# Four blocks of the second image's attention weights turned by TensorE instead of by a trip through DRAM

## The chip, the cores and the metric

The kernel runs on one core of a Trainium2 chip. The metric is the device time of one execution in microseconds (us), the median over several runs. A core has TensorE (PE, matrix products), VectorE (DVE), ScalarE (ACT), GpSimd (POOL) and SyncE (SP, which here only issues transfers), and 16 DMA engines that all queues share. Matrix products write PSUM banks of 128 x 512 floats; DVE, ACT and POOL carry results on.

## The reference, cut to what matters

Two images of 128 channels x 64 x 64 pixels, that is 4096 tokens of 128 channels each, go through a neighbourhood-attention layer (layer 0) and then through layer 1, whose first half is full self-attention in which queries, keys and values are the same normalised tokens:

```python
sim = jnp.einsum('blh,bmh->blm', q, q) * scale
sim = jnp.where(diag[None, :, :], jnp.float32(-1000000000.0), sim)
attn = jax.nn.softmax(sim, axis=-1)
return jnp.einsum('blm,bmh->blh', attn, q)
```

The second half of layer 1 is a spectral convolution: filters `phi`, branch matrices `M_phi_plus` and `M_phi_minus` (four branches of 16 matrices of 128 x 128 each, mixed with weights from a softmax) and `M_u` for three short lags. All of it is in float32.

## The kernel before, in words

**Order.** Layer 0 of both images comes first, in an order written out by a planner. Then `attention(0, fill)` and `attention(1, fill)` do the self-attention of the first and of the second image, and the convolution's long loop ends the kernel. This case lies in `attention(1)`, at about 800 to 1250 us of the profile.

**Pairs of chunks.** The 4096 tokens are cut into 8 chunks of 512. Since queries and keys are the same tokens, the block of exponentials E for queries in chunk a and keys in chunk c is the transpose of the block for queries in c and keys in a. So only the 36 pairs with a <= c are computed. For a pair off the diagonal, `weights` computes four row tiles of 128 x 512 (scores on PE in L927 or L936, exponential on ACT in L932 or L943); then
- `other` (L1057): E itself, contracted over the tokens of a, is added to the result of chunk c;
- `own` (L985): E transposed, contracted over the tokens of c, is added to the result of chunk a. This needs E turned.

**Two ways to turn.** A "far" pair is turned by way of DRAM: ACT issues one 1 MB store `eb<-e` (`sent`, L959), two steps later SP issues four loads `et<-eb` of 256 KB (`moved`, L966), which put 32 x 32 blocks into place, and DVE turns inside the blocks with two stream transposes of 128 x 1024 (`turned`, L975). The four `own` products follow eight steps after the store (`DELAY`). The pair (6, 7), the last one, is not far: after each of its four `other` products PE turns four 128 x 128 tiles into a PSUM bank (`turned_here`, L981), DVE copies the bank out (L982), and `own` follows one step later.

**Steps and fillers.** A pair off the diagonal takes four steps. In a step PE does a score product for the next pair, an `other` product of this pair and up to two `own` products that are due (`late`, a first-in first-out list), and `fill()` adds one piece of unrelated work. The order is written by hand for PE, DVE, ACT, POOL and SP: nothing is reordered at run time. In the second image the fillers are, in this order: what is left of the first image's tokens (`after`: it ends with 12 stores `us<-ub` per chunk, four of 128 KB and eight small ones of 32 KB, L1094, each after an addition on POOL, L1141); whenever a chunk is complete, `after` for that chunk; and `for_ffn`, which loads the branch matrices (`filter_matrices`: 32 loads `st` of 256 KB, issued by SP at L1277 about three ahead of use and added up on DVE in L1299 and L1301), then the table `inv` (320 KB, L1499, scaled on DVE in L1501) and the first blocks `ct` and `ut` of the convolution (L1459, L1467).

**Completion counters.** The framework gives each DMA one of eight completion counters in turn; SP's and ACT's DMAs draw from the same eight. Before a queue issues a DMA it waits until the DMA that last held this counter has landed. So a store on SP may have to wait for an `eb` store of ACT that drew the same counter.

**Buffers.** `e` and `et` have two buffers each (1 MB), `eb` four, the PSUM ring `bank` five, `own` two, `other` one.

Of the kernel before, what the change touches and what calls it, by code (L numbers as in the profile page):

```python
# [92 lines left out]
CHUNKS = (0, 1, 4, 5, 2, 3, 6, 7)  # L93
# [9 lines left out]
def kernel(  # L103
# [136 lines left out]
    with l0a:  # L240
# [551 lines left out]
        for k, (b, g) in enumerate(order):  # L792
            t = {}
# [83 lines left out]
    with ap_:  # L877
# [24 lines left out]
        def attention(b, fill):  # L902
# [8 lines left out]


            pairs = [(a, c) for a in range(8) for c in range(a, 8)]
            far = lambda a, c: a != c and (a, c) != (6, 7)
            chunk = lambda a: slice(CHUNKS[a] * 512, (CHUNKS[a] + 1) * 512)

            def weights(a, c, k, left, halves):
# [66 lines left out]
            def onto(own, n, out_, e, first, last):  # L984
                nc.tensor.matmul(out_, lhsT=tok[b][:, n, :], rhs=e, start=first, stop=last, skip_group_check=True)  # L985

            def complete(a, own):
                xs = xa[b][:, chunk(a)]
                if a:
                    nc.vector.tensor_tensor(xs, own, xs, ALU.add)  # L990
                else:
                    nc.vector.tensor_copy(xs, own)
                fill(CHUNKS[a])

            def pair_onto(own, a, c, et, t):
                if (a, c) == (6, 7):
                    onto(own, 4 * CHUNKS[c] + t, own, et[:, t], False, t == 3)
                    if t == 3:
                        complete(a, own)
                    return  # L1000
                onto(
                    own, 4 * CHUNKS[c] + t, own.rearrange("p (k q i) -> p q k i", k=4, q=4),
                    et.rearrange("p q (k t i) -> p t q k i", k=4, t=4)[:, t], False, c == 7 and t == 3,
                )
                if (c, t) == (7, 3):
                    complete(a, own)
# [11 lines left out]
            def pass_on(n):  # L1018

                while coming_ and coming_[0][0] + MOVE <= step:  # L1020
                    at, eb, a, c = coming_.pop(0)
                    et = moved(eb)
                    turns.append((at + TURN, et))
                    late.extend((at + DELAY, a, c, et, t) for t in range(4))
                while turns and turns[0][0] <= step:
                    turned(turns.pop(0)[1])
                while n and late and late[0][0] <= step:
                    _, a, c, et, t = late.pop(0)
                    pair_onto(owns[a], a, c, et, t)
                    n -= 1  # L1030
# [409 lines left out]
        kept = []  # L1440
        fill, left = filler(0, steps, kept)
        attention(0, fill)
        for gen in steps:
            for _ in gen:
# [63 lines left out]
        kept = []  # L1508
        fill, left = filler(1, steps, kept)
        attention(1, fill)  # L1510
        adder[:] = [nc.vector]
        for gen in steps:
# [23 lines left out]
    with ExitStack() as cv:  # L1536
# [201 lines left out]
        b = NB - 1  # L1738
# [117 lines left out]
```

## Time and profile before

| | us |
|---|---|
| median of 3 runs | 2059.06 (2057.91 to 2060.68) |
| the profiled execution | 2061.56 |
| its span, first to last instruction | 2059.8 |
| PE busy | 1924.6 (93%) |
| DVE, ACT, POOL busy | 941.0, 733.1, 570.6 |
| TensorE clock granted, mean | 0.971 of full |

The span is the time from the first to the last instruction of the profiled execution; 1.8 us of that execution lie around it. Matrix products overlap at their ends, so a stretch in which PE is "busy" is not free of small gaps, but an idle time in front of a product, which the timeline shows in brackets with its releaser, is real. In a timeline a product of 128 x 512 floats is two instructions (x2), which start 0.86 us before the next product does when PE is not held up.

### The profile page before, as it was taken

What the parts mean: (1) busy time and instruction counts of PE and PEld (TensorE: products, weight loads), DVE (VectorE), ACT (ScalarE), POOL (GpSimd) and SP (SyncE); (2) the same over time, 40 slices, a digit from 0 to 9 for tenths busy, and PEclk for the clock granted to TensorE, in tenths of its full rate; (3) what the DMA queues carried; (4) which work ended last, traced back from release to release, by engine and by line L of the source; (5) the groups of instructions that cost most, each with busy time, mean ns of one, the idle gap of its engine ahead of it and who ended that gap; (6) DMA issues with size and microseconds to landing.
All of it is one profiled execution on the core that took longest, in us unless ns stands there. A gap on an engine that the chain in (4) does not pass through costs nothing.

```text
span 2059.8 us, 50961 instructions
## 1 busy us (share of the span) xinstructions
PE 1924.6 (93%) x20504; PEld 1355.8 (66%) x20504; DVE 941.0 (46%) x2918; ACT 733.1 (36%) x1718; POOL 570.6 (28%) x954
## 2 busy tenths in 40 slices
PE   6899998999899999897978898999999999999998
PEld 4677775444444444443433344799999899999987
DVE  5799995443544343242533336333333334333332
ACT  3789885312223323222312232222222222222222
POOL 4467986303422113101101111022222121222211
PEclk8999999999999999999989999999999999999999
DMA  5222221667656534648865632222222123222211
GB/s 153 62 62 62 62 58 31 191 149 232 188 154 178 159 108 150 172 119 209 226 173 160 182 112 73 70 68 67 66 67 60 51 56 103 68 66 67 67 45 43
DMA packets 278378, 225.97 MB, mean 110 GB/s; under 512 B 122607, under 2 KB 241535, under 8 KB 270720
## 3 DMA queue, kind: packets, MB, share of 16 engines
q1 hardware_dynamic: 269442, 162.59, 32.1%
q10 hardware_dynamic: 8126, 58.04, 7.0%
q8 instruction: 163, 2.67, 0.5%
q0 software_dynamic: 576, 2.10, 0.3%
q14 instruction: 71, 0.58, 0.1%
HBM read 131.40 MB, written 91.25 MB: 108 GB/s over the span
## 4 chain that ended last, share of the span: by engine, by line
PE 75%; DVE 8%; DMA 5%; POOL 4%; issue 4%; ACT 1%; SPq 1%; DVEq 0%; POOLq 0%; ACTq 0%
PE acc L1584 27%; PE own L985 10%; PE bank L927 7%; PE pc L1565 7%; PE other L1057 6%; PE bank L349 2%; PE bank L559 2%; PE bank L202 2%; PE bank L1156 2%; DMA et<-eb 2%; PE bank L1199 1%; DMA eb<-e 1%; DVE et L975 1%; PE bank L523 1%; PE po L581 1%
## 5 line engine op out<-in xcount | busy, mean ns | idle before, releaser
L1570 DVE COPY y<-pc 128x512 f32<-128x512 f32 x320 | 206.1, 686 | 347.4 <-PE pc L1565 345.9
L1584 PE MATMUL acc<-y,mpl 32*128 32x256 f32 x5120 | 324.9, 380 | 0.8 <-DVE af L1594 0.8
L1584 PE MATMUL acc<-y,mmi 32*128 32x256 f32 x5120 | 316.5, 375 | 0.0
L1570 ACT COPY y<-pc 128x512 f32<-128x512 f32 x320 | 171.9, 589 | 392.7 <-PE pc L1565 379.1
L1584 PEld LDWEIGHTS acc<-y,mpl 32*128 32x128 f32 x5120 | 289.9, 186 | 8.3 <-DVE af L1594 1.3
L1584 PEld LDWEIGHTS acc<-y,mmi 32*128 32x128 f32 x5120 | 290.9, 185 | 3.9
L985 PE MATMUL own<-et,tok 128*128 128x512 f32 x448 | 225.9, 629 | 61.2 <-DVE et L975 49.1
L932 ACT ACTIVATE e<-bank 128x512 f32<-128x512 f32 x216 | 128.8, 599 | 308.0 <-PE bank L927 302.7
L1057 PE MATMUL other<-e,tok 128*128 128x512 f32 x448 | 230.9, 597 | 6.5 <-DVE xa L1066 6.5
L927 PE MATMUL bank<-cm 128*128 128x512 f32 x432 | 227.3, 608 | 0.0
L1565 PE MATMUL pc<-ct,ut 32*128 32x256 f32 x2560 | 212.5, 377 | 3.1 <-DVE y L1570 3.1
L1595 POOL TENSOR_TENSOR af<-af 128x512 f32<-128x512 f32 x39 | 49.7, 1275 | 589.2 <-DVE af L1594 589.2
L985 PEld LDWEIGHTS own<-et,tok 128*128 128x128 f32 x448 | 86.9, 199 | 177.5 <-issue 108.7
L1565 PEld LDWEIGHTS pc<-ct,ut 32*128 32x128 f32 x2560 | 172.7, 186 | 9.3 <-DVE y L1570 5.2
L975 DVE STREAM_TRANSPOSE et<-et 128x1024 f32<-128x1024 f32 x108 | 127.7, 1221 | 67.6 <-DMA et<-eb 66.3
L174 POOL TENSOR_TENSOR ln_rs<-ln_rs,mhalf 128x4 f32<-128x4 f32 x24 | 25.3, 1054 | 480.6 <-DVE ln_rs L173 480.5
L1057 PEld LDWEIGHTS other<-e,tok 128*128 128x128 f32 x448 | 81.6, 191 | 100.0 <-issue 84.0
L1141 POOL TENSOR_TENSOR ub<-uo 128x256 f32<-128x256 f32 (+1 forms) x160 | 96.5, 640 | 178.1 <-ACT uo L1138 167.5
L927 PEld LDWEIGHTS bank<-cm 128*128 128x128 f32 x432 | 76.9, 194 | 73.5 <-issue 67.8
L546 ACT ACTIVATE p<-p,mn 128x196 f32<-128x196 f32 x256 | 114.4, 449 | 14.4 <-DVE mn L536 13.8
L1138 ACT COPY uo<-bank 128x512 f32<-128x512 f32 (+1 forms) x96 | 46.9, 517 | 125.3 <-PE bank L1156 96.6
L943 ACT ACTIVATE e<-bank 128x512 f32<-128x512 f32 (+1 forms) x72 | 32.6, 455 | 139.0 <-DVE bank L941 133.9
(261 smaller groups left out, 2559.7 us busy)
## 6 DMA issues: line engine op xcount, KB each, us to landing
eb<-e ACTq DMA_DIRECT2D x54, 1024.0 KB
et<-eb SPq DMA_DIRECT2D x216, 256.0 KB
ut<-us SPq DMA_DIRECT2D x160, 128.0 KB
us<-ub SPq DMA_DIRECT2D x128, 128.0 KB
ct<-gs SPq DMA_DIRECT2D x320, 40.0 KB
vw<-vd SPq DMA_DIRECT2D x256, 49.0 KB
ct<-gs SPq DMA_DIRECT2D x320, 32.0 KB
vd<-v SPq DMA_DIRECT2D x128, 32.0 KB
```

The costliest lines, as they stand in the source:

```text
L546: nc.scalar.activation(p, p, AF.Exp, bias=t[name + "mn"][:, h : h + 1], scale=-1.0, accum_out=t["den"][:, u, h : h + 1],)
L927: nc.tensor.matmul(ps.rearrange("p (q t j) -> p q t j", q=4, t=4), lhsT=cm[b][:, n * P : (n + 1) * P], rhs=keys.rearrange("p (t q j) -> p ...
L932: nc.scalar.activation(e, ps.rearrange("p (q r) -> p q r", q=4), AF.Exp, bias=0.0, scale=ASCALE)
L975: in_place(nc.vector.transpose(flat, flat))
L985: nc.tensor.matmul(out_, lhsT=tok[b][:, n, :], rhs=e, start=first, stop=last, skip_group_check=True)
L1057: nc.tensor.matmul(turn(other, "p (q r) -> p q r"), lhsT=tok[b][:, n, :], rhs=es[j], start=(j == 0), stop=(j == 3),)
L1138: nc.scalar.copy(both[:, 0 : 2 * n], pu[s][:, 0 : 2 * n])
L1141: adder[0].tensor_tensor(ub[:, sgn, 0:n], both[:, 0:n], both[:, n : 2 * n], op)
L1565: nc.tensor.matmul(pcs[j].rearrange("p (g o c) -> p o g c", g=4, o=2)[:, :, at], lhsT=ut[rows_, par, :], rhs=cv_[rows_], start=True, stop= ...
L1570: (nc.scalar.copy if j % 2 else nc.vector.tensor_copy)(y[:, :, :, 4 * kl + j, :], pcs[j].rearrange("p (g x k) -> p k g x", g=4, k=KF))
L1584: nc.tensor.matmul(acc[j][:, 0:256], lhsT=(mmi if l else mpl)[rows_, k, :], rhs=y[rows_, k, 2 * l : 2 * l + 2].rearrange("p s n x -> p (s ...
L1595: eng.tensor_tensor(af[:, 0:2], af[:, 0:2], af[:, 2:4], ALU.add)
```

## The change

The set of pairs that are turned on the spot grows, for the second image only. `pairs[9:27:3]` are the entries 9, 12, 15, 18, 21 and 24 of the list of pairs: (1, 2), (1, 5), (2, 2), (2, 5), (3, 3) and (3, 6). The pairs (2, 2) and (3, 3) are on the diagonal and were never far, so four pairs change their way: (1, 2), (1, 5), (2, 5) and (3, 6). For each of them the `eb` store, the four `et` loads and the two stream transposes go, and 16 turns of 128 x 128 on PE and four copies of 128 x 512 on DVE come. Their `own` products come one step after each turn, or as soon as an older far pair in `late` has been served, instead of eight steps after a store; scores and exponentials are laid out in plain order.

```diff
             pairs = [(a, c) for a in range(8) for c in range(a, 8)]
-            far = lambda a, c: a != c and (a, c) != (6, 7)
+            here_ = {(6, 7), *(pairs[9:27:3] if b else ())}
+            far = lambda a, c: a != c and (a, c) not in here_
...
             def pair_onto(own, a, c, et, t):
-                if (a, c) == (6, 7):
-                    onto(own, 4 * CHUNKS[c] + t, own, et[:, t], False, t == 3)
-                    if t == 3:
+                if not far(a, c):
+                    onto(own, 4 * CHUNKS[c] + t, own, et[:, t], False, c == 7 and t == 3)
+                    if (c, t) == (7, 3):
                         complete(a, own)
                     return
```

The second hunk lets pairs other than (6, 7) go that way: the sum of chunk a is closed only by its last pair, the one with c = 7.

## The prediction

> **What bounds the kernel now.** I read the page first (PE is busy for 93% of the span, so PE sets the time wherever it isn't kept waiting), then the table by stage, to see where it is kept waiting. Columns: stage, its length, busy us (x instructions) of PE, PEld, DVE, ACT, POOL, granted clock, DMA share, GB/s.
>
> ```profile
> 940.00:1020.00 80.00, 65.69 (x167) 29.61 (x166) 36.16 (x67) 20.53 (x44) 3.15 (x4) 0.94 0.83 214
> 1020.00:1070.00 50.00, 35.76 (x104) 16.01 (x103) 19.57 (x31) 10.50 (x24) 5.52 (x10) 0.86 0.74 195
> 1070.00:1110.00 40.00, 32.11 (x80) 14.14 (x79) 16.96 (x39) 11.06 (x23) 2.64 (x3) 0.87 0.51 151
> 1110.00:1150.00 40.00, 32.27 (x98) 14.56 (x97) 7.99 (x13) 7.56 (x15) 6.01 (x11) 0.90 0.63 172
> ```
>
> In these 210 us, the middle of the second image's attention, PE is idle for 44 us and the DMA engines are at their busiest. PE's timeline shows where: four long stalls, each in front of an `own` product on a turned block: **A** at 949.8 (11.46 us), **B** at 1038.7 (12.44), **C** at 1095.5 (6.85), **D** at 1139.7 (7.16). What ends them stands in the chain of work that ended last (start, us, what):
>
> ```profile
> 949.59 5.10 DMA eb<-e
> 955.72 3.10 DMA st<-in_m_plus_dram
> 959.99 1.22 DVE et L975
> 961.25 3.58 PE own L985 x4
> ...
> 1038.50 3.88 DMA eb<-e
> 1045.58 3.15 DMA st<-in_m_minus_dram
> 1049.87 1.22 DVE et L975
> 1051.13 3.78 PE own L985 x4
> ...
> 1092.38 6.62 DMA inv<-t_out
> 1100.01 2.28 DVE et L975 x2
> 1102.34 3.78 PE own L985 x4
> ...
> 1118.70 5.12 DMA eb<-e
> 1136.77 3.88 DMA et<-eb
> 1140.67 6.21 DMA ct<-gs
> 1146.88 3.77 PE own L985 x4
> ```
>
> The reader is to see that A and B wait not for the turned block but for a branch matrix: DVE stands at `mpl` or `mmi` (L1299) until `st` lands, and the stream transposes are queued behind it. `st` is late because SP is. The waits of SP from 940 to 1150:
>
> ```profile
> SPq L1094 <- DMA eb<-e: 28.5, 5, 6.7
> ```
>
> SP's small `us` stores share completion counters with ACT's `eb` stores. In the listing of waits of the built program, one of A's last stores has the counter of (1, 6)'s `eb`, issued at 949.59; one of B's has that of (2, 6), and one of the last three that of (2, 7), issued at 1038.50. In A: `eb` lands at 954.7, SP goes on, `st` is issued at 955.3 and lands at 958.4, DVE needs 0.5 and 2.4 us, PE starts at 961.25. C waits for `inv`, queued on SP behind the four loads of (3, 5). In D the loads of (3, 7) are queued behind 15 `ct` and `ut` loads, and these behind a store with the counter of (3, 7)'s `eb` (1118.70).
>
> Each stall also costs the clock: after B four products take 3.57 us from start to start and not 1.72, the next 1.71 and not 0.86: about 2.8 us with the rest; the same after C and D, 1.7 after A.
>
> **What the Trainium skill says.** (1) "TensorE: Matmul & The Clock Gate", Part 1: an idle window of about 3.4 us halves the clock; the products at twice their time after A to D agree. (2) The same page, Part 4: a turn on PE ends in PSUM and needs a DVE copy. The trace agrees: 273 ns for a turn, and each bank is copied in 686 ns; back to back the turns cost less, as the next fence shows. (3) "DMA: Bandwidth & Descriptors", Issuing engines are not separate DMA queues: transfers of ACT and SP run on the same 16 engines. That fits the loads and stores that overlap here, and is why I expect fewer bytes to help a little, but none of the four stalls is a lack of bandwidth alone.
>
> **The change part by part.** PE, DVE, ACT, SP (POOL's order is unchanged; so is all of the first image):
>
> *Added on PE:* 4 pairs x 16 turns. Four of them take 0.43 us of PE (start to start):
>
> ```profile
> 1230.91 0.60 PE L981 MATMUL bank<-ident,e 128*128 128x128 f32 x4
> 1231.34 0.81 PE L936 MATMUL bank<-cm 128*128 128x384 f32 x2
> ```
>
> 16 x 0.43 = **6.9 us**, less the last 0.4 us of (1, 5), which fall into stall A: **+6.5**. Nothing hides the rest, as PE is the bound.
>
> *Added and removed on DVE:* 16 copies x 0.686 = 11.0 us against 8 stream transposes x 1.214 = 9.7 us. DVE is busy for under half of these stages, so the time itself is covered by PE's; but each copy stands in DVE's order, with an `own` product behind it, and a fifth of the PSUM ring is held until it is done. In (2, 5) and (3, 6) each step then takes four banks of the five rather than three. No row shows this; the nearest is the last pair, where turns on the spot made PE wait 1.42 us once (1241.8). Bounds: 0 (no wait) to 16 steps x 0.25 us = 4; below nothing it can't be. I take **+1.5**.
>
> *Removed from the queues:* ACT loses 4 issues of 0.33 us, SP 16 of 0.43 us = 6.8 us. Both queues have idle time, so this counts only through what it lets pass. *Removed from the DMA engines:* 4 x 2 MB. The scores and exponentials stay as many, of the same size.
>
> *Stall A:* in the new order of waits (1, 6)'s `eb` again holds the counter of a small `us` store, now the last but one of the chunk. The stall stays: `eb` may land 1.2 us sooner (3.8 us after (1, 1), when the engines were quiet, against 5.1), but one more issue (0.55) and one copy of (1, 5) (0.6) now lie between it and PE. I take **-0.5**, bounds -3 and +2.
>
> *Stall B:* in the new order none of the 12 stores of that chunk draws an `eb`'s counter; (2, 6)'s `eb` falls behind them and its next holder is a load of its own block. So `st` no longer waits for (2, 7). POOL's last addition ended at 1027.5 there; eight issues of 0.55 us, 0.9 us of shift and a landing of 3.2 us give about 1036, where DVE waits, with only the sum of (2, 6), due at 1040, behind it. The pair for which PE waited, (2, 5), is turned by PE itself. **-12.44 - 2.8 = -15.2.** What could be late next is C.
>
> *Stall C:* (3, 5) stays far, `inv` stays behind it. Only (3, 6)'s `eb` (issued at 1095.38) leaves the engines while `inv` lands: **-1**, bounds 0 and -9.6 (all of it and the clock).
>
> *Stall D:* no `us` store draws (3, 7)'s counter now; a `ct` load does, 6 issues later, when that `eb` has landed. `ct` starts about 4.2 us sooner (1123 and not 1127.2), and so do the four loads of (3, 7) at 1136.77; with (4, 5)'s `eb` of 1139.52 no longer beside them they should land some 3 us faster than the 7.6 us they took. Both together are as much as the stall: **-7.16 - 2.7 = -9.9**, bounds -3 and -9.9.
>
> Sum: 6.5 + 1.5 - 0.5 - 15.2 - 1 - 9.9 = **-18.6 us** on the profiled execution's 2061.56, so 2043.0; the median of the runs lies 2.5 us under that execution: **2040.5**.
>
> **The rivals.**
> 1. *B and D go, A and C stay* (as above): 2040.5; with the bounds of its terms 2036 to 2053. For it: the counters in the listing and the landing times fit A, B and D to a tenth of a us.
> 2. *Bandwidth was the cause, and A and C go too:* 2 MB less in every third pair. It would bring up to 13.2 + 9.7 us more, less the 1.5 counted: some 2019; half of it 2030. For it: the DMA share of 0.83 from 940 on. Against: from 945.5 to 949, just ahead of A, the engines move 15 to 46 GB/s, the small stores alone.
> 3. *The stall moves:* B's work comes 15 us sooner, the branch matrices don't, and DVE stops at another `st` or at `inv` with a copy or a transpose behind it. Then C grows by up to what B and D lose: 2052 to 2059. For it: DMA share 0.74 with PE stalled; it must run the same loads in less time.
> 4. *Slower:* the copies are the new wait. Every turned pair has its four `own` products behind DVE copies, and DVE stands at L1299 or L1301 for `st`; if in (2, 5) and (3, 6) it stands as long as before, B and D survive with PE waiting for a copy, and the turns (6.9) and the ring (4) are paid for nothing: 2070. It decides once the stalls shrink by less than 8 us in sum. Against: in the new DVE order the copies of (2, 5) stand ahead of the `mmi` at which B stood.
> 5. *It doesn't do what it says:* six entries are picked and two are diagonal pairs; the built program shows 64 more turns, 16 fewer loads and 4 fewer stores, so four pairs are changed.
>
> **How the numbers follow.** Chances: rival 1 0.61, rival 2 0.15, rival 3 0.13, rival 4 0.11. A measurement of this kernel can tell about 0.2%, 4.1 us, from no change. Rivals 1, 2 and two thirds of 3 are faster by more: 0.84; a third of 3 is within: 0.05; slower 0.11. The range leaves out rival 4 and the far half of rival 2: 2027 to 2057.
>
> **What would show it right or wrong.** In the profile after: 96 turns on the spot (32 now), `et<-eb` x200, `eb<-e` x50. A stall of 10 to 12 us at the end of (1, 5), still ended by `st` and behind SP's wait for an `eb`; none over 3 us after (2, 6); one of 5 to 7 us ended by `inv` after (3, 5); at most 3 us after (4, 4). SP's wait of L1094 for `eb` falls from 28.5 to under 15 us. I am wrong if PE waits for L982 for more than 5 us in sum, if B comes back under another `st`, or if A is gone too.

## Result: 2050.6 us against 2058.3, less than half of the forecast gain

In runs taken in turn on one chip the kernel before had a median of 2058.3 us (2055.95 to 2060.68) and the changed kernel 2050.63 us (2048.89 to 2054.29): a ratio of **0.996, 95% interval 0.9947 to 0.9973**, that is 7.7 us less. The forecast was 18.6 us less. The profiled execution of the changed kernel took 2050.63 us, its span is 2048.9 us, and PE's granted clock is 0.977 (before: 0.971). Behind the edited line the numbers of the changed kernel's lines are one higher: L985 of the kernel before is L986, L1094 is L1095; some experiments move them again.

**The same four stages after the change** (columns as before: stage, length, busy us of PE, PEld, DVE, ACT, POOL, granted clock, DMA share, GB/s):

```profile
940.00:1020.00 80.00, 65.76 (x179) 30.24 (x177) 35.96 (x68) 18.91 (x41) 1.45 (x1) 0.94 0.70 185
1020.00:1070.00 50.00, 45.44 (x146) 21.36 (x143) 22.94 (x35) 13.98 (x30) 7.22 (x12) 1.00 0.69 182
1070.00:1110.00 40.00, 32.02 (x105) 14.66 (x104) 13.88 (x36) 11.88 (x26) 7.78 (x11) 0.87 0.46 127
1110.00:1150.00 40.00, 34.96 (x91) 16.27 (x90) 11.02 (x19) 6.28 (x13) 0.88 (x3) 0.91 0.55 147
```

The second stage is another one: PE busy for 45.4 us and not 35.8, at the full clock. That is where B was. In the fourth, where D is, PE is busy for 35.0 us and not 32.3. In the first stage the DMA share falls from 0.83 to 0.70, and PE is busy for 65.8 us against 65.7 before: the fewer bytes brought nothing there.

**The stalls.** PE's timeline (start, us, what, and in brackets the idle time just before it and its releaser; x4 are four instructions, two products of 128 x 512, which the prediction calls four products) has these left in place of A to D:

```profile
963.45 3.78 PE L986 MATMUL own<-et,tok 128*128 128x512 f32 x4 [11.38 <-DVE et L976]
1033.72 1.98 PE L986 MATMUL own<-et,tok 128*128 128x512 f32 x4 [0.90 <-DVE et L976]
1053.38 0.33 PE L950 MATMUL bank<-ident,e 128*128 128x128 f32 x1 [1.53 <-ACT e L944]
1057.12 0.33 PE L950 MATMUL bank<-ident,e 128*128 128x128 f32 x1 [2.11 <-ACT e L944]
1094.90 3.78 PE L986 MATMUL own<-et,tok 128*128 128x512 f32 x4 [6.95 <-DVE et L976]
1114.03 1.98 PE L986 MATMUL own<-et,tok 128*128 128x512 f32 x4 [0.90 <-DVE et L976]
1138.42 2.07 PE L986 MATMUL own<-et,tok 128*128 128x512 f32 x2 [4.14 <-DMA ct<-gs]
```

A (11.38) and C (6.95) are as they were, B is gone, D is 4.14 and not 7.16. (The profile names a `ct` load as D's releaser, since it came last; the stream transposes for which the product waits ended at 1138.37, 0.05 us ahead of it.) New are two waits of 0.90 us in the last steps of (2, 5) and (3, 6), for the stream transposes (L976) of the far pair before, and 1.84 us more of waiting for exponentials at the diagonal pair (3, 3) (1.53 + 2.11, where the kernel before has 1.80). The counts are as forecast:

```profile
L982 PE MATMUL bank<-ident,e 128*128 128x128 f32 x96 | 14.4, 273 | 0.0
eb<-e ACTq DMA_DIRECT2D x50, 1024.0 KB
et<-eb SPq DMA_DIRECT2D x200, 256.0 KB
```

**What SP waits for**, from 940 to 1150 (us, times, longest):

```profile
SPq L1095 <- POOL ub L1142: 33.1, 18, 16.6
SPq L1095 <- DMA eb<-e: 10.2, 1, 10.2
```

The waits of small `us` stores for an `eb` fell from 28.5 us to one of 10.2, the one of stall A. Between 1020 and 1050, around B, the kernel before waited 11.7 us for `eb` stores and 1.0 us for POOL's sums; now it is 0 and 11.9. SP reaches the stores sooner and waits for the engine that makes their data.

**Where the time went.** The two profiled executions, cut at the products that end the stalls:

| stretch | before | after | difference | forecast |
|---|---|---|---|---|
| start to the product at 896 | 896.64 | 896.05 | -0.6 | 0 |
| to the product after A | 64.61 | 67.40 | +2.8 | +3.3 |
| to the product after C (holds B) | 141.09 | 131.45 | -9.6 | -14.1 |
| to the product after D | 44.53 | 43.52 | -1.0 | -5.1 |
| to the last wait of the last pair | 94.92 | 95.36 | +0.4 | -2.7 |
| to the end of the span | 818.01 | 815.12 | -2.9 | 0 |
| sum | | | -10.9 | -18.6 |

The clock that the end of D was to bring back (2.7 us) stands in the row behind D, where its products run. The first and the last row lie outside the change; these two executions differ by 3.5 us there. The four rows between add up to -7.4 us, near the 7.7 by which the medians differ.

### The profile page after: what moved, and what is told of

The parts are those of the page before. It is cut to its first block, busy times and chain, and to the rows that moved or that the text cites. A ratio compares the mean times of both kernels' runs of the same rounds, so it can differ in the third digit from the quotient of the medians.

```text
span 2048.9 us, 51053 instructions
## 1 busy us (share of the span) xinstructions
PE 1926.2 (94%) x20568; PEld 1361.6 (66%) x20568; DVE 942.6 (46%) x2926; ACT 732.9 (36%) x1718; POOL 570.4 (28%) x954
## 4 chain that ended last, share of the span: by engine, by line
PE 61%; issue 21%; DVE 6%; POOL 6%; DMA 4%; SPq 1%; ACT 1%; POOLq 0%; DVEq 0%; ACTq 0%
PE acc L1585 27%; PE pc L1566 7%; PE own L986 5%; PE bank L928 4%; PE other L1058 3%; PE bank L349 2%; POOL ub L1142 2%; PE bank L559 2%; PE bank L202 1%; DMA et<-eb 1%; PE bank L523 1%; PE po L581 1%; DMA us<-ub 1%; PE pc L1624 1%; PE bank L344 1%
## 5 line engine op out<-in xcount | busy, mean ns | idle before, releaser
L986 PE MATMUL own<-et,tok 128*128 128x512 f32 x448 | 224.6, 625 | 47.0 <-DVE et L976 37.8
L933 ACT ACTIVATE e<-bank 128x512 f32<-128x512 f32 x200 | 119.6, 599 | 308.6 <-PE bank L928 303.5
L928 PE MATMUL bank<-cm 128*128 128x512 f32 x400 | 209.8, 606 | 0.0
L986 PEld LDWEIGHTS own<-et,tok 128*128 128x128 f32 x448 | 86.1, 198 | 159.6 <-issue 105.9
L1142 POOL TENSOR_TENSOR ub<-uo 128x256 f32<-128x256 f32 (+1 forms) x160 | 96.4, 636 | 179.9 <-ACT uo L1139 169.5
L976 DVE STREAM_TRANSPOSE et<-et 128x1024 f32<-128x1024 f32 x100 | 118.3, 1221 | 56.2 <-DMA et<-eb 47.4
L928 PEld LDWEIGHTS bank<-cm 128*128 128x128 f32 x400 | 70.3, 193 | 63.8 <-issue 58.5
L944 ACT ACTIVATE e<-bank 128x512 f32<-128x512 f32 (+1 forms) x88 | 41.7, 480 | 131.5 <-DVE bank L942 121.3
```

The lines of the kernel that those rows point to most:

```text
L928: nc.tensor.matmul(ps.rearrange("p (q t j) -> p q t j", q=4, t=4), lhsT=cm[b][:, n * P : (n + 1) * P], rhs=keys.rearrange("p (t q j) -> p ...
L933: nc.scalar.activation(e, ps.rearrange("p (q r) -> p q r", q=4), AF.Exp, bias=0.0, scale=ASCALE)
L976: in_place(nc.vector.transpose(flat, flat))
L1142: adder[0].tensor_tensor(ub[:, sgn, 0:n], both[:, 0:n], both[:, n : 2 * n], op)
```

## Experiments

The label of each run stands with its result. All ratios are to the kernel before, run in turn with the experiment on the same chip. Two theories stand against each other: **the queue's order** (PE waits since SP, and behind it DVE, stand at something in their order) and **the bytes** (the DMA engines are too busy).

### One pair alone: (2, 5)

```diff
-            here_ = {(6, 7), *(pairs[9:27:3] if b else ())}
+            here_ = {(6, 7), *(((2, 5),) if b else ())}
```

> Only the pair (2, 5) is turned on the spot; (1, 2), (1, 5) and (3, 6) go by way of DRAM as before. In the listing of waits (2, 7)'s store is then followed, eight transfers later, by a load of its own block and no longer by a small us store, as in the changed kernel; the counters around A and D fall as in the kernel before (last small store, third small store). Counter theory: stall B goes, A (11 us), C (7) and D (7) stay; the stretch from A's end to C's end shrinks by about the 10.1 us that it shrank by in the changed kernel, nothing else changes: about 2048, that is below the changed kernel. Bandwidth theory (fewer bytes are what counts): a quarter of the bytes brings a quarter of the 7.7 us: about 2056.

Measured (p25): ratio 0.9973 (0.9963 to 0.9984), 5.6 us less. In the timeline of PE B is gone, and A, C and D stand as before (C 1.1 and D 0.8 us longer):

```profile
960.46 3.78 PE L986 MATMUL own<-et,tok 128*128 128x512 f32 x4 [10.97 <-DVE et L976]
1030.49 1.98 PE L986 MATMUL own<-et,tok 128*128 128x512 f32 x4 [0.91 <-DVE et L976]
1093.11 3.78 PE L986 MATMUL own<-et,tok 128*128 128x512 f32 x4 [7.93 <-DVE et L976]
1137.76 2.93 PE L986 MATMUL own<-et,tok 128*128 128x512 f32 x3 [7.92 <-DMA ct<-gs]
```

From A's end to C's it saves 8.4 us (132.65 and not 141.09), near the 9.6 of the whole change. So B belongs to this one pair. The edit does two things at once: SP no longer waits for that counter, and PE no longer needs this pair's stream transposes; no run splits them. The gain was expected 5 us larger than it came out: the waits at C and D are 1.8 us longer, and behind the last pair's wait the profiled execution takes 4.5 us more than the kernel before (see the next run).

### Two pairs alone: (1, 2) and (1, 5)

```diff
+            here_ = {(6, 7), *(((1, 2), (1, 5)) if b else ())}
```

> Only the pairs (1, 2) and (1, 5) are turned on the spot. The stores of B and D meet the counters of (2, 6), (2, 7) and (3, 7) as before. Counter theory: A, B, C and D all stay within 1 us of before; the two pairs cost what the stretch up to A's end cost more in the changed kernel, 2.8 us: about 2061, slower than before. Bandwidth theory: half of the bytes, half of the gain: about 2054.

Measured (p12_15): ratio 1.0041 (1.0027 to 1.0056), 8.4 us **slower**. All four stalls stay (11.61, 11.94, 7.81, 7.89). From 896 to A's end it takes 67.62 us, 3.0 more than before, as two pairs of turns should. But the loss is larger than that: 1.4 us from A to C, and 4.8 us between the last pair's wait and the convolution's first product on `y`. That last stretch took 60.7 to 66.9 us in the profiles of this study, in no order that follows from an edit (61.2 before, 60.7 after, 66.1 here). Here it begins with DVE waiting 1.29 us for a `us` store at an addition (L1142, 1257.15), a wait that the kernel before doesn't have; PE's wait for `z` is then 4.38 us and not 3.00, and later waits grow too. Why that store is late was not tried and stays open. It is one reason why the parts don't add up to the whole; (3, 6) alone was not tried. That these two pairs bring nothing by themselves is beyond the interval.

### The traffic put back

```diff
+            def traffic(a, c, i):
+                big = dram.tile([P, 2048], F32, tag=f"big{a}{c}{i}", name="big")
+                nc.gpsimd.dma_start(out=big, in_=m_plus[i].rearrange("k (h d) e -> (k h) (d e)", h=8))
...
```

(Left out: the two places where it is called.)

> The changed kernel with the traffic put back that it saved: for each of the four pairs POOL issues one copy of 1 MB from DRAM to DRAM where the store was issued and one where the loads were; nothing waits for them, they draw no counter of SP and ACT, and the counters stand as in the changed kernel up to the end of C. Counter theory: as the changed kernel within 2 us, B stays gone: 2049 to 2053. Bandwidth theory: B comes back at 8 us or more and A and C grow: 2058 or more.

Measured (bytes): ratio 1.0001 (0.999 to 1.0012): the whole gain is gone again. Yet B did not come back:

```profile
965.54 3.37 PE L986 MATMUL own<-et,tok 128*128 128x512 f32 x4 [12.16 <-DVE et L976]
1035.38 1.98 PE L986 MATMUL own<-et,tok 128*128 128x512 f32 x4 [0.90 <-DVE et L976]
1101.19 3.78 PE L986 MATMUL own<-et,tok 128*128 128x512 f32 x4 [9.35 <-DVE et L976]
1144.98 3.78 PE L986 MATMUL own<-et,tok 128*128 128x512 f32 x4 [5.19 <-DMA ct<-gs]
```

Both theories are half right. B is not a matter of bytes. But with the copies the waits for other transfers are longer (A by 0.8, C by 2.4, D by 1.05 us against the changed kernel, 4.2 us in sum). C and D had stayed at most at 7.26 and 4.14 us in every run of the changed kernel without the copies. The profiled execution is 11.7 us longer than the changed kernel's, and 6.1 of these lie behind the last pair's wait, where stretches differ anyway; so only the 4.2 us are seen to be a price. The engines move as many bytes as in the kernel before (225.97 MB in both), but not the same transfers: the copies read and write DRAM alike, so DRAM reads and writes are each 4.2 MB above the kernel before, the copies take fewer packets than the traffic they stand for, and POOL spends about 0.5 us on the issue of each. That other traffic has a price for the waits that are left, which my sum had at next to nothing, is shown; its size for the saved traffic is not.

### The queue relieved, no pair changed

```diff
-                nc.sync.dma_start(out=to, in_=src)
+                (nc.gpsimd if by_pool and src.shape[0] == 64 else nc.sync).dma_start(out=to, in_=src)
```

(`by_pool` is set during the second image's attention; `src.shape[0] == 64` picks the small stores.)

> The kernel before, no pair more turned on the spot, all bytes moved; the eight small us stores (32 KB each) of every chunk in the second image's attention are issued by POOL, which makes their data, and not by SP. POOL's transfers have counters of their own, and since eight are taken out of the round of eight, every other transfer keeps its counter. (2, 7)'s counter then comes to a load of (2, 6) behind the st loads, (1, 6)'s to a load or st behind the first three. Counter theory: A and B go (11.5 + 1.7 and 12.4 + 2.8 us), less up to 6 us for what is late next; C stays; D stays or shrinks by half: about 2035, range 2028 to 2044. Bandwidth theory: the same bytes compete at the same time, A and B stay: 2056 to 2060.

Measured (before_pool): ratio 0.9917 (0.9901 to 0.9933), 17 us less, with every byte moved and no turn added. The first lines of PE, around A, and those at B, C and D:

```profile
943.84 1.98 PE L985 MATMUL own<-et,tok 128*128 128x512 f32 x4 [2.13 <-DVE et L975]
958.14 2.07 PE L985 MATMUL own<-et,tok 128*128 128x512 f32 x2 [3.74 <-DVE et L975]
1028.96 2.08 PE L985 MATMUL own<-et,tok 128*128 128x512 f32 x2 [2.58 <-DVE et L975]
1042.08 0.47 PE L949 MATMUL bank<-ident,e 128*128 128x128 f32 x1 [4.12 <-ACT e L943]
1083.58 3.40 PE L985 MATMUL own<-et,tok 128*128 128x512 f32 x4 [6.91 <-DVE et L975]
1123.42 3.22 PE L985 MATMUL own<-et,tok 128*128 128x512 f32 x4 [3.71 <-DVE et L975]
```

A is 2.13 + 3.74 and not 11.46, B 2.58 and not 12.44 although (2, 5) still goes by way of DRAM. SP's own line shows why:

```profile
937.90 1.48 SPq L1277 DMA_DIRECT2D st<-in_m_plus_dram  x3
```

In the kernel before these loads were issued from 955.3 on; this execution runs 8.1 us ahead at the product at 896, so SP is 9.3 us sooner. This run takes two things off SP, the waits for `eb` counters and eight issues per chunk, and doesn't split them. Not all of the 17 us lie at A and B: an earlier wait in the second image's attention, for stream transposes at 829.55 (6.89 us in the kernel before, 7.04 in the changed one), which the prediction doesn't name, is 3.91 us here, and 3.65 to 4.41 us in all runs in which POOL issues the small stores. The rest of the 8.1 us was there before the edit could act (5.4 us at the last pair of the first image).

### Undo D and C by order alone

In the changed kernel, the `ct` and `ut` loads three steps later:

```diff
-            yield
+            for _ in range(4):
+                yield
             yield from load_blocks()
```

> The changed kernel with one thing moved: the ct and ut loads of the convolution's first blocks start three steps later, so the four et loads of (3, 7) stand ahead of all of them in SP's order and not behind 15 of them. Theory (D is SP's order: the issues of 15 loads, 12 us from 1115.5 to 1127.4, stand ahead of the loads for which PE waits): D's 4.1 us and its lost clock go, 4 to 6 us less: ratio to before about 0.994 (the changed kernel has 0.996). Rival (the et loads land late since the engines are full): D stays at 3 us or more.

Measured (d_only): ratio 0.9919 (0.9903 to 0.9936). D is gone; from C to the last wait it takes 131.7 us and not 138.9, 7.2 us less, where 4 to 6 were expected. What SP does in the changed kernel, and then in this run (start, us from the first to the last issue, what):

```profile
1115.54 4.98 SPq L1460 DMA_DIRECT2D ct<-gs  x4
...
1127.53 1.79 SPq L967 DMA_DIRECT2D et<-eb  x4
1129.36 3.37 SPq L1460 DMA_DIRECT2D ct<-gs  x4
```

```profile
1115.91 2.76 SPq L967 DMA_DIRECT2D et<-eb  x4
1118.71 2.52 SPq L1460 DMA_DIRECT2D ct<-gs  x4
```

The same loads, 11.6 us sooner, of which 3.1 us are this execution's lead at C. The other edit, also in the changed kernel: the load of `inv` and the block loads stay where they are, and the scaling comes two steps later.

```diff
+            first_ones = load_blocks()
+            for _ in range(2):
+                yield
+                next(first_ones)
             for s, (lo, hi) in enumerate(((0, CQ // 8), ...)):
                 nc.vector.tensor_scalar(inv[:, :, lo:hi], ...)
             yield
-            yield from load_blocks()
+            yield from first_ones
```

> The changed kernel with one thing moved: the four DVE instructions that scale inv come two steps after its load and not right behind it; the load stays where it was, and no other transfer moves. Theory (C is DVE standing at inv with stream transposes queued behind it): C's 6.95 us and 2 to 2.8 us of clock go, some 9 us less: ratio to before about 0.992. Rival (the stream transposes of (3, 5) are late by themselves, for lack of bandwidth): C stays at 4 us or more.

Measured (c_only): ratio 0.9906 (0.989 to 0.9921). C's 6.95 us are gone, D's 4.14 become 2.95. DVE now does the copies and stream transposes first, and `inv` behind them without a wait:

```profile
1103.55 2.36 DVE L976 STREAM_TRANSPOSE et<-et 128x1024 f32<-128x1024 f32 x2
1105.84 0.65 DVE L1067 TENSOR_TENSOR xa<-other,xa 128x512 f32<-128x512 f32 x1
1106.41 0.67 DVE L983 COPY et<-bank 128x512 f32<-128x512 f32 x1
1107.01 0.96 DVE L1506 TENSOR_SCALAR inv<-inv,seg 128x80 f32<-128x80 f32 x4
```

### Is the change worth anything once the order is right?

The changed kernel with the small stores issued by POOL:

> The changed kernel with the small us stores issued by POOL, as in the run before_pool. Theory: A and B are then gone without the change, and what is left of the change is its price: four pairs at 1.72 us of turns and about 0.9 us in which own waits for the first copy, 10 us, less what D gains (3 us or less): 3 to 10 us slower than before_pool, ratio to before 0.993 to 0.9965. Rival (fewer bytes help wherever they are taken away): faster than before_pool, ratio below 0.991.

Measured (after_pool): ratio 0.9847 (0.9828 to 0.9866). The rival has the number: the change brings 0.7% (14 us) over before_pool, and 0.4% by itself; the difference is just outside what the intervals allow. Between 900 and 1200 us only C is left of the long stalls:

```profile
951.38 1.99 PE L986 MATMUL own<-et,tok 128*128 128x512 f32 x4 [0.91 <-DVE et L976]
1019.84 1.98 PE L986 MATMUL own<-et,tok 128*128 128x512 f32 x4 [0.91 <-DVE et L976]
1079.30 3.78 PE L986 MATMUL own<-et,tok 128*128 128x512 f32 x4 [7.26 <-DVE et L976]
```

My theory forgot what before_pool still waits for: 5.9 us at A, 2.6 and some 3 at B and behind it, 3.7 at D. They are gone here. At A and B PE no longer needs the DRAM blocks of (1, 5) and (2, 5); that less traffic ahead of the loads that are left helps too is likely, but no run shows it by itself.

The kernel before with all three moves of order (small stores by POOL, `inv` scaled two steps later, `ct` and `ut` behind the `et` loads of (3, 7)):

> The kernel before, all pairs by way of DRAM but (6, 7), with the three moves together: small us stores issued by POOL, inv scaled two steps after its load, ct and ut loads after the et loads of (3, 7). Theory: all four stalls are waits of a queue's order, and all go: 2042 less 6.9 + 2.8 (C) and 3.7 + 1.5 (D), about 2028, ratio 0.985 (0.983 to 0.989). Rival (something else is late next): 0.989 to 0.992.

Measured (pool_cd): ratio 0.9876 (0.9858 to 0.9895). The number lies in the theory's range, but the theory had all stalls go, and waits of 1.86, 3.83, 2.51, 3.89 and 3.40 us are left. These three moves of order don't remove them all.

Four pairs turned on the spot where nothing waits for DRAM:

```diff
+            here_ = {(6, 7), *(((4, 6), (4, 7), (5, 6), (5, 7)) if b else ())}
```

> The kernel before with four other pairs turned on the spot: (4, 6), (4, 7), (5, 6) and (5, 7), from 1150 us on, where no own product waits for DRAM; (1, 2), (1, 5), (2, 5) and (3, 6) go by way of DRAM. As many bytes go as in the changed kernel; A, B, C and D stay. This measures the price of a turned pair alone: 1.72 us of turns and up to 0.9 us of own waiting for the first copy, 4 x 1.7 to 2.6 = 7 to 10.5 us slower, ratio 1.0033 to 1.005. Rival (taking bytes away pays anywhere): no slower than before.

Measured (quiet4): ratio 1.0016 (1.0008 to 1.0025), 3.3 us slower. The turns themselves cost what they should, 0.44 us for four:

```profile
1180.30 0.60 PE L982 MATMUL bank<-ident,e 128*128 128x128 f32 x4
1180.74 1.88 PE L986 MATMUL own<-et,tok 128*128 128x512 f32 x4
```

16 x 0.43 = 6.9 us were paid, and three waits near the end of the attention that the kernel before has (1.42 us for the last pair's copy, 3.00 and 2.33 us at L202 for `z`) are absent here, while one of 1.21 us for `xa` is new and a later one is 2.6 us longer (3.88). So the turns of a pair cost 1.7 us, and there was hardly a wait to add to it (0.47 us at 1166, for transposes). Taking bytes away where nothing waits for them did not pay for the turns.

### Three versions that beat both kernels, one of them without POOL

> The changed kernel with the small us stores issued by POOL and inv scaled two steps after its load. The run after_pool had one long stall left, C (7.26 us, ended by the stream transposes behind inv). Theory: C and its clock go, 9 to 10 us: ratio 0.980 (0.978 to 0.982), the fastest so far. Rival (the next wait takes C's place): 0.983 or more.

Measured (pool_c; both edits shown above): ratio **0.9814 (0.9795 to 0.9833)**, 2021.2 us beside 2060.1 of the kernel before. Between 900 and 1200 us no wait of PE is over 2.11 us.

> As pool_c, but only (1, 5) and (2, 5) are turned on the spot, and the ct and ut loads come after the et loads of (3, 7). In before_pool the waits left at A and B are for these two pairs and for what stands behind them on DVE; (1, 2) and (3, 6) pay turns and save nothing that the order of the queue doesn't save too. Theory: 2 x 1.7 to 2.6 us faster than pool_c: ratio 0.977 to 0.979. Rival (the bytes of (1, 2) and (3, 6) matter too): slower than pool_c.

Measured (pool_2cd): 0.9815 (0.9797 to 0.9833), not faster than pool_c and not slower. The profiles show more: at the last pair's wait this version is 3.9 us ahead (1195.42 and not 1199.29), as the theory says, and it loses 3.8 us behind it, where DVE waits 1.50 us for a `us` store and PE then 4.60 us for `z` and not 3.01, as in the run with (1, 2) and (1, 5). So it is open whether (1, 2) and (3, 6) are worth turning; the two versions also differ in the order of the `ct` and `ut` loads.

> The changed kernel, all stores on SP, with three moves: DVE takes the first branch matrix four steps later (so st has time to land and (1, 6)'s et loads go first), inv is scaled two steps after its load, ct and ut loads come after (3, 7)'s et loads. Theory: A (11.4 + 1.7), C (6.95 + 2.8) and D (4.1 + 1) go: 27 us under the changed kernel, ratio 0.983. Rival: the branch matrices, four steps later, meet the next chunk's us stores, and B or C come back in part: 0.987 to 0.991.

```diff
             for _ in range(3):
                 load()
                 yield
+            for _ in range(4):
+                yield
             for k0, dst, src, i in parts_:
```

Measured (acd; with the moves of C and D): ratio 0.9859 (0.9838 to 0.988). A is gone without POOL issuing anything, and the moves of C and D alone leave it (11.59 and 11.38 us). So A was DVE standing at a branch matrix that need not be used yet. Waits of 1.55, 2.17 and 2.93 us come in its place; the result lies between the two expectations.

## Why the prediction was wrong, point by point

- **The bound.** Right. PE waited in DVE's and SP's order: A went when the first use of `st` was moved as well (acd), C when only the scaling of `inv` was moved (c_only), D when only the block loads were moved (d_only). For B the order was not moved by itself.
- **Turns, +6.5, and ring and copies, +1.5.** About right. The stretch with two turned pairs and an unchanged A grew by 2.8 us (3.3 forecast), by 3.0 in p12_15. PE waited 0.90 us in the last steps of (2, 5) and of (3, 6), not for a copy but for the stream transposes of the far pair before. They stand in DVE's order right behind the third copy, and that copy waits for PE's third group of turns (1030.69, then the transposes from 1031.30 to 1033.66); no term named this. The two waits make 1.8 us, where the sum had 1.5. Two of the expectations above call them waits for the first copy; that was a misreading.
- **A, -0.5.** Right: 11.46 became 11.38. The counter of (1, 6)'s store cost SP 10.2 us in one wait.
- **B, -15.2: the first step that was mis-sized.** The mechanism was right, its size wasn't. The 12.44 us went, in p25 by (2, 5) alone, and the traffic put back didn't bring them back. But DVE stood at the first `st` of `mmi` until 1042.1 and not until about 1036 (about 1038 in this execution, which is 2.7 us later there, 0.9 of which the forecast had). POOL's last sum ended at 1030.6, about as late as that shift makes it, and SP issued `st` at 1035.5. The term that failed is the landing: 6.6 us from this issue to its use, where I had 3.2 and the kernel before has 3.9 (1044.37 to 1048.31).

```profile
1035.50 4.34 SPq L1278 DMA_DIRECT2D st<-in_m_minus_dram  x3
1042.13 0.49 DVE L1300 TENSOR_SCALAR mmi<-st,wt 128x512 f32<-128x512 f32 x1 [5.19 <-DMA st<-in_m_minus_dram]
```

  In p25 it is 6.9 us. Why it is longer there was not tried. It also allows an estimate of what the counters alone did: relative to PE this first `st` came 8.9 us sooner than before (6.2 us and the shift of 2.7), so some 9 of the 12.44 us are SP's, and the rest went because PE turns (2, 5) itself. The matrices stay late, and 1.84 us of it come out again at the diagonal pair (3, 3): the mask that its exponentials need (L942) is queued on DVE behind a matrix for which it waits 2.52 us.

```profile
1051.84 0.75 DVE L1302 SCALAR_TENSOR_TENSOR mmi<-st,wt,mmi 128x512 f32<-128x512 f32 x1 [2.52 <-DMA st<-in_m_minus_dram]
1052.51 0.29 DVE L942 TENSOR_TENSOR bank<-bank,ndiag 128x128 f32<-128x128 f32 x1
```

  The stretch adds up: -12.44 + 1.72 (turns) + 0.90 (transposes behind a copy) + 1.84 + 0.10 (C) = -7.9; the measured -9.6 leaves about -1.8 for the clock, where I had -2.8.
- **C, -1.** It did not shrink: 6.85 became 6.95. With the traffic put back it went up, to 9.35.
- **D, -9.9: the step that failed.** SP issued the loads of (3, 7) sooner, as said: 6.8 us ahead of PE's reaching the product (1127.53 to 1134.28), where it had been 2.9 (1136.77 to 1139.7). But "some 3 us faster" was wrong. From the first issue to the stream transposes it took 8.5 us, and 7.7 before. The engines were full while most of the loads landed (columns as in the stages):

```profile
1127.50:1131.00 3.50, 3.50 (x9) 1.52 (x8) 0.65 (x1) 1.19 (x2) 0.00 (x0) 1.00 0.78 189
1131.00:1136.00 5.00, 3.28 (x8) 1.14 (x6) 0.00 (x1) 1.19 (x2) 0.00 (x0) 1.00 1.03 243
```

  The store of (4, 5) was away for most of that time: ACT issued it 6.6 us after the first load (1134.09), and 2.8 us after it in the kernel before. In c_only it came 7.2 us after the first load, and the loads still took 7.9 us. So that store was not what held them. SP's next `ct` and `ut` loads, issued right behind, are a likely reason; no run held them back by themselves. So 4.14 us stayed; with the turns (1.72), the transposes behind a copy (0.90) and a wait of 0.57 us that is gone, the stretch gained 1.0 us, not 5.1. I had counted "both together are as much as the stall" at its full size: two estimates, one of them with no row behind it, that had to add up to the whole stall, and then the clock on top. The lower bound, -3, is what the wait lost. The clock was not regained: after the 4.14 us the next two instructions took 2.07 us, where 1.02 is usual.
- **The rivals.** None came true as written; it was rival 1 without D. The change did what it says (rival 5). A and C did not go with the bytes (rival 2), but the bytes have a price (the traffic put back). The stall did not move to C, but the 1.84 us at (3, 3), behind another `st`, are a small piece of rival 3; PE waited for a copy itself only at the last pair, 1.42 us as before, and 1.8 us for transposes behind copies (rival 4). Of the signs, the counts, A, C and SP's wait for `eb` came as said; the stall after (4, 4), at most 3 us in the forecast, did not.
- **The sum.** B's stretch fell short by 4.5 us, D's by 4.1 and the clock behind it by 3.1; A's came out 0.5 better. That is 11.2 us of the 18.6 forecast and leaves the 7.4 of the table.

## What to carry to other kernels

When several queues share a bound, ask of each stall which instruction stands at the head of the queue that is late, and whether it has to stand there: moving the use of `inv`, `st` and `ct` by two to four steps brought 1% more (0.9859 and not 0.996), where turning four blocks on another engine had brought 0.4%. A stall that is only shortened may keep its lost clock (D at 4.14 us), and a gain that needs two estimates to cancel it exactly should be entered at its lower bound. A queue that is freed from one wait runs into the next ones (here POOL's sums, and then a landing of 6.6 us), so ask for each of these dates before you count the gain.

## What the runs showed that I had not expected

- A wait for another queue's transfer, through a shared counter, cost up to 10.2 us at once, for a store of 32 KB that has nothing to do with it. With the small stores issued by POOL, which frees SP of these waits and of the issues, the kernel took 17 us less.
- Four loads of 256 KB took 8.5 us to land at a DMA share of 1.03 and 243 GB/s, with small `ct` and `ut` loads issued right behind them in the same queue.
- The clock is lost sooner than I took it to be. The Trainium skill ("TensorE: Matmul & The Clock Gate", Part 1) gives an idle window of about 3.4 us. Here four instructions of `own` ran on at full speed after waits of 1.86 us (pool_cd) and 2.17 us (acd), 1.98 us for the four, and at about half after waits of 2.51 us (pool_cd, 3.48 us) and 2.93 us (acd, 3.78 us). The measured numbers decide. One of each, from acd and from pool_cd:

```profile
1053.44 1.98 PE L986 MATMUL own<-et,tok 128*128 128x512 f32 x4 [2.17 <-DVE et L976]
1031.59 3.48 PE L985 MATMUL own<-et,tok 128*128 128x512 f32 x4 [2.51 <-DVE et L975]
```

- The same change was worth 8 us in a queue that is late (ratio 0.996) and 14 us where the queue had been relieved (0.9847 against 0.9917), though the two differ by little more than the intervals.
